# Attention and a spectral layer on four pictures: from pairs of pictures to single pictures cut in halves

## The chip, the cores and the metric

The kernel runs on one core of a Trainium2 chip. The metric is the device time of one execution in microseconds (us); of the kernel before there are three runs, with a median of 3028.91 us (3028.34 to 3029.63). The engines are PE (TensorE, matrix multiplication; PEld is its loading of weights), DVE (VectorE), ACT (ScalarE), POOL (GpSimd) and SP, which here only issues transfers.

## The reference

The input x has 4 pictures of 64 channels and 96 x 96 = 9216 pixels. All is float32. Two layers follow one another.

```python
# layer 0: x = x + scale * (attention(gn(x)) + gn(x))
q, k, v = wq x + bq, wk x + bk, wv x + bv        # 8, 8 and 64 channels
att = sigmoid(q^T k)                             # 9216 x 9216, per picture
out = v att^T + x                                # x: normalised in groups of 2 channels
scale = sigmoid(mlp(mean(out)) + mlp(max(out)))  # one number per picture and channel
# layer 1: x = x + irfft2(mix(rfft2(gn(x))))
# only 32 rows (16 lowest, 16 highest) x 16 columns of the spectrum are kept;
# each of these 512 frequencies has its own complex 64 x 64 matrix, the same for all pictures
```

The attention matrix is never stored. It has 4 x 9216 x 9216 elements, and this is nearly all of the work.

## The kernel before

**Layout.** Two pictures make a pair: 2 x 64 channels lie on the 128 partitions, and 9216 pixels along the free dimension (`xs[p]`, p = 0, 1). Queries go in blocks of 512 pixels (`NB`), 18 a pair (`NBLK`), so 36 in all. Keys go in chunks of 128 pixels, 72 a picture. A tile is 128 keys of one picture against 512 queries: 144 tiles a block (`TILES`), 5184 in all (`ALL`).

**Stream.** For each tile TensorE makes energies (`energies`, L580: 32 rows by 128 columns against 512 queries, in float32r, with key and query each split in a high and a low part), ScalarE takes the sigmoid (`sigmoids`, L601, several banks of PSUM at once), and TensorE multiplies with the values (`attend`, L618). L618 adds up a block of 64 channels per picture over 144 tiles in one bank; at the end of a block VectorE adds the result to x (L624) and takes its maximum (L626).

**The planner.** The order on the engines is written out. A loop at L805 to L877 makes bursts of up to seven tiles. In turn t the program issues the energies of burst t+1, then the values matmuls of about one burst before. Other work is hung into the turns: a step in `together` uses banks that the burst has just freed (L907, `values_of`, `keys`, `back_h`, `back_w`), a step in `alone` gets one of the two accumulating banks, and the next burst then has six tiles (L894, for `along_w`, `along_h`, `mixing`, statistics). `ends` holds what follows at the end of a turn: vector work and transfers. Where a block changes (`edges`) the burst also has six. `follow` (L718) is a queue of steps that must keep a distance of some turns.

**Keys, queries and values.** `values_of` (L489) makes, for 512 pixels of both pictures, the values and the transposed queries and keys; it has 32 matmul instructions. The parts of keys and queries are turned on VectorE (L537), sent to DRAM by SP (L541) and fetched again: queries by SP (L558), keys by POOL into `stage` (L550), from where VectorE copies them into `kT` (L552). `kT` has 18 slices of 8 tiles. The first 12 slices (`DIRECT`) of the first pair are made by TensorE itself (`keys`, L486). The second pair's values go through 9 turns with two `values_of` each, in the last block of the first pair.

**Ahead of the stream.** SP loads x in pieces of 512 KB, VectorE takes statistics of 18 blocks of the first pair (L632), normalises the first blocks (L170), and TensorE makes the first keys and queries.

**Layer 1 of the first pair** runs hidden in the stream of the second (`Hidden`, L289). In `result` the layer's input is formed in 12 strips of 8 lines; it goes to DRAM and comes back turned (`turned`). `along_w` (6 steps) is the transform along a line, `along_h` (one for each picture) along a column. `mix` (L217) multiplies each kept frequency with its matrix: pictures, real and imaginary part stand on the side that is loaded into TensorE (32 columns), and the matrices are streamed, 16 steps. `back` fetches the result in another order through DRAM, `back_h` (4 steps) and `back_w` (12 steps) are the inverse transforms.

**Layer 1 of the second pair** lies behind the stream (L928 on). From the gate on: 12 strips (L183 combine, L991 transpose, L1003 along the line, some strips added by a transfer, `ADDED`), statistics, rows in three groups (L1009, L1015), the spectrum with its scaling (L1050 to L1066), mixing of the 32 weight rows (L230; 9 come early in the stream, 6 in places free in time, 17 after the stream), `pick` (L261) which brings the last two row groups to their place by matmuls, the addition L274, the inverse along a column (L1105, L1112) and along a line (L1122), the last addition (L1130) and the output (L1131). `occupy` (L958) issues matmuls without use, so that TensorE is busy where it would wait.

Of the kernel before, what the change touches and what calls it, by code (L numbers as in the profile page):

```python
# [43 lines left out]
NPAIR = B // 2  # L44
# [5 lines left out]
NBLK = N // NB  # L50
# [7 lines left out]
ALL = NPAIR * NBLK * TILES  # L58
# [3 lines left out]
U = KH * KW * 4  # L62
UPAD = 4 * SIDE
# [3 lines left out]
NSTRIP = N // STRIP  # L67
ADDED = (4, 5, 6, 8, 10)
# [6 lines left out]
SECOND = {"w1": 2 * R, "w2": P, "ident": P, "fw": 2 * KW, "fh": 4 * KH, "gh": 2 * H, "gw": 4 * W}  # L75
# [7 lines left out]
NLATE = 3 * NSQ * P  # L83
NPICK = 2
PICK = P + 4 * (NPICK - 1)
# [3 lines left out]
def tile_kernel(ctx: ExitStack, tc: tile.TileContext, x, cst, late, spec, out):  # L89
    nc = tc.nc  # L90
    xf = x.rearrange("b c h w -> (b c) (h w)")
    outf = out.rearrange("b c h w -> (b c) (h w)")
# [8 lines left out]
    for p in range(NPAIR):  # L101
        xt = xpool.tile([P, N], F32, tag=f"x{p}", name=f"x{p}")
        for s in range(9):
            parts = 2 if p == 0 and s == 8 else 1
            for i in range(parts):
                cols = bass.ts(parts * s + i, N // 9 // parts)
                nc.sync.dma_start(xt[:, cols], xf[bass.ts(p, P), cols])
        if p == 0:
            nc.sync.dma_start(cs[:, :NFIRST], cst[:, :NFIRST])
        xs.append(xt)  # L110
    nc.sync.dma_start(cs[:, NFIRST:], cst[:, NFIRST:])

    vT = xpool.tile([P, NCH, P], F32, tag="vT", name="vT")
# [4 lines left out]
    pav, nhalf, low_sb, ident = named("pav"), named("nhalf"), named("low"), named("ident")  # L118
# [10 lines left out]
    def group_stats(stats, bank, name):  # L129
# [3 lines left out]
        mr = small.tile([P, 2], F32, tag=f"mr_{name}", name=f"mr_{name}")  # L133
        t = small.tile([P, 1], F32, tag="t", name=f"t_{name}")
        d = small.tile([P, 1], F32, tag="d", name=f"d_{name}")
# [36 lines left out]
    class Layer1:  # L172


        def __init__(self, p, gate, bank, move, queues):
            self.p, self.gate, self.bank, self.move, self.queues = p, gate, bank, move, queues
            self.vd = dram.tile([KH, 32, KW * C], F32, tag=f"vd{p}", name=f"vd_{p}")
            self.vt = None

        def combine(self, s, old):  # L180

            cols = bass.ts(s, STRIP)
            nc.vector.scalar_tensor_tensor(xs[self.p][:, cols], xs[self.p][:, cols], self.gate,  # L183
                                           old, ALU.mult, ALU.add)

        def spread(self, mr):


            p = self.p
            self.rs = small.tile([P, 3, 2], F32, tag="rs", name=f"rs_{p}")  # L190
            pr = self.bank(f"pr_{p}")
            for b in range(2):
                for part in range(2):
                    self.last = nc.tensor.matmul(pr[bass.ts(part, C), bass.ts(b, 2)],
                                                 ident[:, bass.ts(b, C)], mr,
                                                 start=True, stop=True)
            v = pr[:, :4].rearrange("q (b t) -> q t b", t=2)
            m = small.tile([P, 2], F32, tag="m", name=f"m_{p}")
            if p == 0:
                nc.vector.tensor_scalar(m, v[:, 0, :], float(-H), None, ALU.mult)  # L200
                nc.vector.tensor_copy(self.rs[:, 0, :], v[:, 1, :])
                nc.vector.tensor_scalar(self.rs[:, 1, :], v[:, 1, :], -1.0, None, ALU.mult)
# [7 lines left out]
        def constant_mode(self):  # L210

            for part in range(2):
                rows = bass.ts(part, C)
                at = self.ut[rows, 2 * part:2 * part + 2]
                nc.vector.tensor_tensor(at, at, self.rs[rows, 2, :], ALU.add)
# [1015 lines left out]
```

## Time and profile before

| what | us |
|---|---|
| median of three runs | 3028.91 |
| profiled execution, its time | 3029.19 |
| its span, first to last instruction | 3027.4 |
| first energies (L580) start | 23.4 |
| last values matmul (L618) ends | 2949.8 |
| PE busy | 3009.2 (99%) |
| ACT busy | 2416.8 (80%) |
| DVE busy | 308.1 (10%) |

The page gives busy time of each engine in 40 equal slices, the granted clock of TensorE in tenths, the load of the transfer engines, the chain of work that ended last, and groups of instructions by line. A group's row has the line, engine, operation, tiles and shapes, then the busy time, the mean of one in ns, and the idle time ahead of it with what ended it. A timeline's row has the start, the time, and the instruction with its count. [...]

### The profile page before, as it was taken

Reading aid. Unit: us, or ns where it says so; the run is one execution under the profiler, and the core shown is the slowest. Engines: PE = TensorE matmul, PEld = TensorE weight load, DVE = VectorE, ACT = ScalarE, POOL = GpSimd, SP = SyncE. Lnnn points to the kernel's source line nnn. Section 1 sums busy time; section 2 is a strip of 40 time slices with the busy share of each in tenths; the row PEclk is TensorE's granted clock in tenths of the full one; section 3 lists DMA queues with packets and bytes.
Section 4 is the critical chain, followed back from the end, with each engine's and each line's share of the span. In section 5 each row is a group of like instructions: output and inputs, shape, how many; then the busy total and the mean of one; then the engine's idle time right before and its main releaser. Section 6 shows DMA issues by size and latency. Waiting matters only on the chain.

```text
span 3027.4 us, 44108 instructions
## 1 busy us (share of the span) xinstructions
PE 3009.2 (99%) x19364; PEld 1111.5 (37%) x19364; DVE 308.1 (10%) x706; ACT 2416.8 (80%) x1555; POOL 69.8 (2%) x138
## 2 busy tenths in 40 slices
PE   9999999999999999999999999999999999999998
PEld 4333333333333333333433333333333333333336
DVE  6300000000000000002411101100000000000006
ACT  4788888888888888887788887777778888888873
POOL 0100000000000000001300000000001000000001
PEclk9999999999999999999999999999999999999999
DMA  4100000000000000001422322412113000000027
GB/s 159 32 4 4 4 4 4 4 4 4 2 4 4 4 4 4 4 4 31 99 68 64 91 79 84 135 34 46 50 47 125 4 4 4 4 4 4 1 60 252
DMA packets 114609, 117.09 MB, mean 39 GB/s; under 512 B 77488, under 2 KB 84784, under 8 KB 114320
## 3 DMA queue, kind: packets, MB, share of 16 engines
q1 hardware_dynamic: 105536, 92.82, 11.0%
q0 software_dynamic: 7472, 18.56, 2.0%
q8 instruction: 152, 2.49, 0.3%
q10 hardware_dynamic: 1408, 2.88, 0.3%
q14 instruction: 41, 0.34, 0.0%
HBM read 79.94 MB, written 32.31 MB: 37 GB/s over the span
## 4 chain that ended last, share of the span: by engine, by line
PE 98%; DVE 1%; DMA 0%; ACT 0%; issue 0%; SPq 0%; POOL 0%; DVEq 0%; ACTq 0%
PE banks L618 77%; PE banks L580 17%; PE banks L499 1%; PE banks L230 1%; PE pv L230 0%; DVE x L1130 0%; PE banks L421 0%; DMA x<-in_x_dram 0%; PE pa L1003 0%; ACT at L601 0%; PE banks L344 0%; PE pu L1015 0%; PE banks L464 0%; DVE xt L991 0%; DVE x L183 0%
## 5 line engine op out<-in xcount | busy, mean ns | idle before, releaser
L601 ACT ACTIVATE at<-banks 128x2048 f32<-128x2048 f32 (+1 forms) x1501 | 2388.3, 1642 | 533.7 <-PE banks L580 521.7
L618 PE MATMUL banks<-at,vT 128*64 128x512 f32 (+1 forms) x11824 | 2402.0, 547 | 0.0
L618 PEld LDWEIGHTS banks<-at,vT 128*64 128x64 f32 x11824 | 778.2, 136 | 1362.7 <-issue 1307.6
L580 PE MATMUL banks<-q,kT 32*128 32x512 f32 x5040 | 542.7, 452 | 0.8 <-ACT at L601 0.7
L580 PEld LDWEIGHTS banks<-q,kT 32*128 32x128 f32 x5040 | 223.7, 182 | 447.5 <-issue 333.4
L624 DVE SCALAR_TENSOR_TENSOR x<-banks,x 128x512 f32<-128x512 f32 x36 | 24.9, 691 | 2023.2 <-PE banks L618 1945.3
L550 POOL DMA_DIRECT2D stage<-qk x96 | 47.6, 503 | 932.3 <-DMA qk<-turned 929.1
L425 DVE TENSOR_TENSOR x<-banks,x 128x768 f32<-128x768 f32 x12 | 11.5, 958 | 168.5 <-PE banks L421 168.5
L499 PEld LDWEIGHTS banks<-cs,x 64*64 64x64 f32 x1152 | 21.8, 135 | 17.0 <-ACT at L601 12.8
L506 DVE TENSOR_TENSOR vT<-banks,cs 128x256 f32<-128x256 f32 x72 | 26.8, 413 | 0.0
L499 PE MATMUL banks<-cs,x 64*64 64x80 f32 (+1 forms) x1152 | 25.9, 234 | 0.0
L626 DVE TENSOR_REDUCE maxs<-x 128x1 f32<-128x512 f32 x36 | 24.7, 686 | 1.3
L632 DVE BATCH_NORM_STATS2 stats<-x 128x6 f32<-128x512 f32 x36 | 22.6, 682 | 3.7 <-DMA x<-in_x_dram 3.7
L736 DVE COPY ws<-banks 128x512 f32<-128x512 f32 x16 | 11.1, 691 | 115.3 <-PE banks L230 115.3
L163 POOL TENSOR_TENSOR mr_l<-ve_l,cs 128x1 f32<-128x1 f32 x4 | 2.2, 559 | 837.1 <-DVE ve_l L162 837.1
L736 DVE COPY ae<-banks 128x512 f32<-128x512 f32 x6 | 4.2, 692 | 157.3 <-issue 114.9
L984 POOL DMA_DIRECT2D x<-vT x5 | 4.5, 1035 | 659.5 <-ACT x L983 659.5
L580 PE MATMUL banks<-q_first,kT 32*128 32x512 f32 x144 | 17.3, 463 | 1.8 <-ACT at L601 1.1
L671 PE MATMUL banks<-x 128*128 128x256 f32 (+1 forms) x48 | 14.4, 459 | 4.7 <-DMA x<-in_x_dram 4.7
L537 DVE STREAM_TRANSPOSE turned<-t 128x384 f32<-128x384 f32 (+1 forms) x35 | 17.8, 509 | 1.2
L170 DVE TENSOR_SCALAR x<-x,mr_l 128x512 f32<-128x512 f32 x36 | 17.6, 530 | 0.7 <-POOL mr_l L163 0.7
L1003 PE MATMUL pa<-xt,lc 128*128 128x256 f32 x72 | 16.8, 385 | 0.6 <-DVE mr_l L152 0.4
(145 smaller groups left out, 425.7 us busy)
## 6 DMA issues: line engine op xcount, KB each, us to landing
ws<-in_spec_dram SPq DMA_DIRECT2D x20, 512.0 KB
q<-qk SPq DMA_DIRECT2D x280, 32.0 KB
x<-in_x_dram SPq DMA_DIRECT2D x17, 512.0 KB
out_dram<-x SPq DMA_DIRECT2D x17, 384.0 KB
room<-in_spec_dram SPq DMA_DIRECT2D x12, 512.0 KB
old<-in_x_dram SPq DMA_DIRECT2D x12, 384.0 KB
qk<-turned SPq DMA_DIRECT2D x96, 48.0 KB
x1d<-x SPq DMA_DIRECT2D x12, 384.0 KB
```

Of the source, the lines that this page charges most:

```text
L170: nc.vector.tensor_scalar(dst, src, mr[:, 0:1], mr[:, 1:2], ALU.subtract, ALU.mult)
L230: self.last = nc.tensor.matmul(pv[bass.ts(g, 32), :].rearrange("q (n k o) -> q n k o", n=SIDE, o=C)[:, :, k, :], self.ut[:, at:at + 32], s ...
L499: projected[0] = nc.tensor.matmul(pp[bass.ts(e, P // 2), b, 2 * a + h, :width], src[rows, a, h, bass.ts(e, P // 2)], named("wv")[rows, :wi ...
L506: nc.vector.tensor_tensor(vT[:, 4 * s:4 * s + 4, bass.ts(b, C)].rearrange("p (h a) m -> p a h m", h=2), pp[:, b, :, :C].rearrange("p (a h) ...
L537: nc.vector.transpose(turned[:, k:].rearrange("p k a (m h) -> p (k a) h m", h=2), t[:, k:].rearrange("p k a h m -> p (k a) h m").bitcast(F32))
L550: nc.gpsimd.dma_start(come[bass.ts(r, QK), :], split[p][s][:, r % 2, bass.ts(r // 2, NB // 2)])
L580: nc.tensor.matmul(banks[:, bank_of(i), :], kT[r:r + 32, i % TILES // 8, i // 4 % 2, :], ask[i // TILES][r:r + 32, :], start=True, stop=True)
L601: nc.scalar.activation(at[:, of:of + n, :], banks[:, bank:bank + n, :], AF.Sigmoid)
L618: attended[0] = nc.tensor.matmul(acc[half, cols], vT[:, j, half], at[:, place(2 * pair + b), cols], start=(j == 0), stop=(j == NCH - 1 and ...
L624: nc.vector.scalar_tensor_tensor(blk, acc, 1.0, blk, ALU.mult, ALU.add, accum_out=sums[p][:, m:m + 1])
L626: mark[0] = nc.vector.tensor_reduce(maxs[p][:, m:m + 1], blk, AX.X, ALU.max)
L632: each = [lambda s=s: nc.vector.bn_stats(stats[:, s, :], xs[p][:, bass.ts(s, NB)]) for s in range(NBLK)]
```

## The change

Pictures now go one by one. The upper half of a picture (48 lines) lies on partitions 0 to 63, the lower on 64 to 127, so `xs` has four tiles of 4608 columns. A block is 512 pixels of the upper half and 512 of the lower; there are 9 blocks a picture and 36 in all, each with 144 tiles of 128 keys by 512 queries as before. The key and value chunks of both halves serve both halves' queries.

Ahead of the stream only the first picture's 2.36 MB are loaded and measured, in pieces of 128 KB on SP and ACT, one for each half. Group statistics are averaged over the two halves too. `values_of` takes one block of 512 columns in both halves, that is 16 tiles' keys, and is called 9 times a picture. There are two buffers of values, so that the next picture's are written while the last is read; these calls stand one to a turn in the last block of each picture. A slice of `kT` is 256 columns in both halves, still 8 tiles; two slices come with one `values_of`, and the first 12 of the first picture are made by TensorE.

Layer 1 of pictures 0, 1 and 2 is hidden. After each of them come its gate, 6 strips, three `along_w`, statistics and one `along_h`, while the stream goes on with the next picture. The scaling needs no matmul now (`spread`). The three spectra stand side by side (`n = 3`), and one mixing of 16 steps serves all, in the stream of the last picture; 6 `back_h` and 18 `back_w` follow, three turns apart where they were four. Behind the stream is layer 1 of picture 3 alone: 6 strips, two row groups, one spectrum, a mixing of the same 32 weight rows with one picture, picks of half the width, and 6 strips of output, each written by two transfers. Of the weights 12 rows come early, 6 in places free in time, 4 into a buffer of values as the stream ends, 10 behind the strips. The matrix for the inverse comes ready from the host.

The diff is cut to its core.

```diff
-NBLK = N // NB
+NBLK = HALF // NB
+NKEY = 2 * NBLK
-ADDED = (4, 5, 6, 8, 10)
+ADDED = (4, 5)
+APART, APART_LAST = 6, 4
...
+    for p in range(B):
+        xt = xpool.tile([P, HALF], F32, tag=f"x{p}", name=f"x{p}")
+        step = NB if p == 0 else 3 * NB
+        for s in range(HALF // step):
+            cols = bass.ts(s, step)
+            read(xt[:, cols], p, cols, (nc.sync, nc.scalar if p == 0 else nc.sync))
-    vT = xpool.tile([P, NCH, P], F32, tag="vT", name="vT")
+    vTs = [xpool.tile([P, NCH, C], F32, tag=f"vT{i}", name=f"vT{i}") for i in range(2)]
...
+        def keep(self, q, queue):
+            for g in range(4):
+                queue.dma_start(self.vd[4 * q + g],
+                                self.vms[q][32 * g:32 * g + SIDE * 2 * self.n, :])
...
+        def spread(self, p, mr):
+            rs = self.rs[p] = small.tile([P, 3], F32, tag="rs", name=f"rs_{p}")
+            nc.vector.tensor_copy(rs[:, 0:1], mr[:, 1:2])
...
+        def mixing(self, q, half):
+            self.mix(q, half)
+            if half == 0:
+                return
+            self.keep(q, nc.sync)
+            if q in (5, 7):
+                first, rows = KH // 2 * (q == 7), KH // 2
+                for slot in range(2):
+                    for b in range(2):
+                        self.back(self.vt, 64 * b + 32 * slot, first, rows, b, slot, 0, SIDE, nc.sync)
+                    for n in range(2):
+                        self.back(self.vt2, 64 * n + 32 * slot, first, rows, 2, slot, 2 * n, 2, nc.sync)
...
+        NSTAGE = 8
+        stage = work.tile([P, NSTAGE, NB // 2], F32, tag="stage", name="stage")
...
             for r in range(4):
                 nc.gpsimd.dma_start(come[bass.ts(r, QK), :],
-                                    split[p][s][:, r % 2, bass.ts(r // 2, NB // 2)])
+                                    split[p][s // 2][:, r // 2, bass.ts(s % 2, NB // 2)])
...
             def means():
+                nc.vector.tensor_reduce(f[:, 1:2], maxs[p], AX.X, ALU.max)
+                nc.vector.tensor_copy(top, f[C:, 1:2])
                 nc.vector.tensor_reduce(tot, sums[p], AX.X, ALU.add)
+                nc.vector.tensor_tensor(f[:C, 1:2], f[:C, 1:2], top, ALU.max)
+                nc.vector.tensor_scalar(f[:, 0:1], tot, 1.0 / HALF, None, ALU.mult)
             def hidden():
+                nc.tensor.matmul(ph[:R, 1:2], named("w1", C), f[:C, 1:2], start=True, stop=True)
+                nc.tensor.matmul(ph[:R, 0:1], named("w1"), f[:, 0:1], start=True, stop=True)
...
+            for m in range(NSTRIP // 2):
+                follow(True, lambda m=m: l1.along_w(p, m), 1, 15 + apart * (2 * m + 1))
+            stats = l1.stats_steps(p)
+            follow(None, stats[0])
+            for step in stats[1:3]:
+                follow(True, step, 2)
+            follow(None, lambda: (stats[3](), home(p)), 2)
+            follow(True, lambda: l1.along_h(p), 2)
+            if p < HIDDEN - 1:
+                return
...
+            for i in range(6):
+                follow(2, lambda i=i: l1.back_h(i % 2, i // 2), 4 if i else 4)
+            for b in range(HIDDEN):
+                for s in range(NSTRIP):
+                    follow(2, lambda b=b, s=s: l1.back_w(b, s), 3 if b or s else 9)
...
-                if renewed < NBLK and was >= TILES * (NBLK - 1) + 8 * (renewed + 2):
-                    for s in (renewed, renewed + 1):
-                        steps.append((2, lambda s=s: values_of(1, s)))
-                        arrive(t, 1, s)
-                    renewed += 2
+                p, s = divmod(renewed, NBLK)
+                if p < B and total[t] >= TILES * (NBLK * p - 1) + 16 * (s + 1):
+                    steps.append((2, lambda p=p, s=s: values_of(p, s)))
+                    arrive(t, p, 2 * s)
+                    arrive(t, p, 2 * s + 1)
+                    renewed += 1
...
+        for i in range(4):
+            weight(next(late_rows), last_v[:, bass.ts(i, KW * C)], nc.sync)
...
             var = small.tile([P, 1], F32, tag="var", name="var")
+            rows_turned(0)
+            rows(0)
             nc.vector.tensor_reduce(var, squares, AX.X, ALU.add)
...
+        for s in range(4):
+            weight(next(late_rows), place_of(f"t{s}", f"w_t{s}"), nc.sync)
+        for i in range(4):
+            weight(next(late_rows), again[:, bass.ts(i, KW * C)], nc.sync)
+        for n in range(NGROUP):
+            weight(next(late_rows), place_of(f"a{n}", f"w_a{n}"), nc.sync)
...
+        nc.vector.tensor_tensor(vt, picked, vt, ALU.add)
+        occupy(1, l1.last, mix_bank.tile([P, NB], F32, tag="v", name="idle_v", bufs=6), NB // 2)
...
+                write(p, cols, x1[:, cols], (nc.sync, nc.scalar))
```

## The prediction

> **What bounds the kernel now.** I read the page's busy slices and its chain first, then the timeline of one engine to get the price of a turn, then a table of stages for the end.
>
> ```profile
> PE   9999999999999999999999999999999999999998
> PE 98%; DVE 1%; DMA 0%; ACT 0%; issue 0%; SPq 0%; POOL 0%; DVEq 0%; ACTq 0%
> L618 PE MATMUL banks<-at,vT 128*64 128x512 f32 (+1 forms) x11824 | 2402.0, 547 | 0.0
> ```
>
> TensorE is never free and 98% of the chain is its own. So in the stream nothing is hidden: a step that puts work on TensorE costs its time, and one that only adds DMA, VectorE (10% busy) or GpSimd work costs nothing unless TensorE waits for it. Only ahead of the stream (to 23.4 us) and behind it (from 2949.8 us) do other engines set the pace. The timeline gives the price of a turn (energies of one burst, then the values matmuls of the one before) as the distance between the starts of two bursts:
>
> ```profile
> 2937.22 0.73 PE L580 MATMUL banks<-q,kT 32*128 32x512 f32 x7
> 2941.05 0.73 PE L580 MATMUL banks<-q,kT 32*128 32x512 f32 x7
> ...
> 94.23 0.74 PE L580 MATMUL banks<-q_first,kT 32*128 32x512 f32 x7
> 96.77 0.79 PE L499 MATMUL banks<-cs,x 64*64 64x80 f32 x32
> 98.92 0.73 PE L580 MATMUL banks<-q_first,kT 32*128 32x512 f32 x7
> ...
> 1402.07 0.74 PE L580 MATMUL banks<-q,kT 32*128 32x512 f32 x7
> 1404.61 1.34 PE L499 MATMUL banks<-cs,x 64*64 64x80 f32 x64
> 1407.32 0.73 PE L580 MATMUL banks<-q,kT 32*128 32x512 f32 x7
> ...
> 1564.07 0.73 PE L580 MATMUL banks<-q,kT 32*128 32x512 f32 x6
> 1564.74 1.06 PE L344 MATMUL banks<-xT,cs 96*32 96x512 f32 x8
> 1568.46 0.74 PE L580 MATMUL banks<-q,kT 32*128 32x512 f32 x7
> ```
>
> A plain turn of seven tiles takes 3.82 us. One of six at an edge takes 3.39, so a tile is 0.43 and the fixed part of a turn 0.81. Every step has a price above that: one `values_of` beside the burst 0.87 (98.92 - 94.23 - 3.82), two in one turn 1.44, an `along_w` alone 1.00 (4.39 - 3.39). Read the same way at every turn: `mixing` 1.00, `along_h` 1.85, `back_h` 1.21, `back_w` 0.98, `hidden` and `gates` 0.40 and 0.11, the two statistics steps of layer 0 0.31 each, of layer 1 0.67 and 0.93, `spread` 0.23, keys with values 1.45. Turns with no step at all hold 6.2 us of small stalls together. With these prices the 751 turns add up to the stream.
>
> **The change, part by part.** Work is counted by walking the planner's loop, in the old and the new form.
>
> *Tiles and turns.* 36 query blocks of 144 tiles both times, so the 5184 x 0.43 us stay. 46 steps now take a burst of six for themselves instead of 31, edges stay 35: 753 turns for 751, **+1.6** (2 x 0.81).
>
> *Values and keys of the first image.* The first pair had 18 `values_of` in its first 15 turns, at 21.7 us above plain turns. The first image has 9 (one ahead, eight here). Turns: first two as before (2.8 and 2.3, they wait for ScalarE), four with keys and values (4 x 1.45), four with keys alone (1.45 - 0.87, with the burst's split 0.65 each), two with values alone (0.87): 15.2. **-6.5.**
>
> *Values of the later images.* Before, 18 in nine turns of two: 13.0. After, 27 singles in 27 turns. A single has 0.79 us of matmul, but costs 0.87. 27 x 0.87 = 23.6: **+10.6.** If a single cost only half a pair (0.72) it would be +6.5; I take the measured single.
>
> *Hidden spectral layer.* Three images for two. `along_w` 9 for 6 (+3.0), `along_h` 3 for 2 (+1.9), `back_h` 6 for 4 (+2.4), `back_w` 18 for 12 (+5.9), layer-0 statistics 3 x 2 steps for 2 (+1.2), gates three times with one more tiny matmul (0.15) each (+1.5). Layer-1 statistics run three times, `spread` leaves TensorE. Their one execution came to 1.6 us, but one step waited for a bank at an edge; between 0.31 and 0.93 a step I take 0.5: 3.0 against 1.8, +1.2. `mixing` stays at 16 turns: three images widen the stationary side, not what streams. Together **+17.1** (15 to 20). DMAs: `keep` still issues four per row group, `back` eight for four, each write two for one, all on SP, whose issues take 0.3 to 0.5 us; in the same stage it waits 14 us at a time for weights and no burst suffers.
>
> *Small stalls.* About 0.1 an edge, as now; those behind the one change of pair (turns 366 to 397, 1.8 us) may come three times: **+2.8** (0 to 6).
>
> *Ahead of the stream.*
>
> ```profile
> 4.54 11.46 DVE L632 BATCH_NORM_STATS2 stats<-x 128x6 f32<-128x512 f32 x18 [3.67 <-DMA x<-in_x_dram]
> ...
> 26.00:27.00 1.00, 1.00 (x7) 0.49 (x7) 0.93 (x5) 0.89 (x2) 0.00 (x0) 0.84 1.05 411
> 27.00:28.00 1.00, 1.00 (x4) 0.30 (x4) 0.22 (x1) 1.00 (x2) 0.00 (x0) 0.50 0.56 216
> ```
>
> VectorE works without a gap from 4.54, 0.64 us a block, so 18 blocks end at 16.0. Nine take 5.7. The first piece is a quarter as large (about 0.6 us earlier); loads at the 405 GB/s seen now need 5.8 us for 2.36 MB, and the constants 0.8 more, which arrive together with the last sums, at about 9.8. The chain from there to the first energies (16.0 to 23.4) stays, with 0.2 less in the aggregate. **-6.4** (-5.5 to -7).
> [...] No row here has pieces that small in such numbers, but in the window 3.5 to 20 us pieces of 256 and 512 KB kept 401 to 425 GB/s with many in flight.
>
> *Behind the stream.*
>
> ```profile
> 2949.80:2953.00 3.20, 2.26 (x11) 1.20 (x10) 1.96 (x8) 0.20 (x1) 0.00 (x0) 1.00 0.47 123
> 2953.00:2963.10 10.10, 9.71 (x37) 6.69 (x37) 9.86 (x15) 9.96 (x18) 6.23 (x9) 1.00 0.78 139
> 2963.10:2974.10 11.00, 10.81 (x49) 7.92 (x47) 10.60 (x11) 5.65 (x12) 2.69 (x5) 1.00 1.03 318
> 2974.10:2982.70 8.60, 8.43 (x40) 4.31 (x41) 4.89 (x13) 2.74 (x8) 1.29 (x3) 1.00 1.03 410
> 2982.70:2996.70 14.00, 14.00 (x257) 9.97 (x257) 7.68 (x14) 5.79 (x10) 0.95 (x1) 1.00 0.98 376
> 2996.70:3002.90 6.20, 4.56 (x21) 3.35 (x19) 1.42 (x4) 0.58 (x1) 0.00 (x0) 1.00 0.23 64
> 3002.90:3009.50 6.60, 6.60 (x40) 4.36 (x40) 4.90 (x8) 0.00 (x0) 0.00 (x0) 1.00 0.00 0
> 3009.50:3021.40 11.90, 10.85 (x97) 10.61 (x96) 10.63 (x13) 0.00 (x0) 0.00 (x0) 1.00 0.77 294
> ```
>
> Columns: stage and length, busy time of PE, PEld, DVE, ACT, POOL, clock, DMA share, GB/s.
> Gate: two more VectorE steps of 0.2 and a second small matmul and its step, 3.2 becomes 3.9 (+0.7). Strips 0 to 5 are the second row and stay (10.1). The third row, strips 6 to 11, goes (-11.0). Spectrum (8.6): the first group's transpose (1.2) now lies behind the last strip, two row matmuls of 1.75 us follow each group, one transpose and smaller scalings replace two of each: 8.8 (+0.2). Mixing streams the same weights: 14.0. Fourteen weight rows load behind the stream for seventeen, 7.3 MB, 18 us at 410 GB/s; the last are wanted 37 us in. Picking (6.2): one addition of 0.69 for four (1.42), and half the matmuls: 5.2. Back along h (6.6): half the matmuls and four transposes of 0.62: 4.3. Strips (11.9, 0.82 to 0.95 each): 6.2. The writes run at 394 GB/s and end 6.0 us behind the last addition, where they are backed up; 2.36 MB need 6.0 us from the first and the same 2.9 of finishing, so 5.2. Sum of the last four: 30.7 becomes 20.9, -9.8. Together **-19.9** (-17 to -22).
>
> **Sum:** +1.6 - 6.5 + 10.6 + 17.1 + 2.8 - 6.4 - 19.9 = -0.7 us on the profiled execution's 3029.19 (span 3027.4 and 1.8 around it): 3028.5. The median of the runs shown is 0.3 below that execution, so I forecast a median of **3028.2**. The bounds of the terms, not all at one end, make it 3022.5 to 3034. What is taken off both ends is paid back in the stream, because the third hidden image and the single `values_of` lie on the engine that is full.
>
> **Where a clock rule bears.** The two rows at 26 and 27 us show the granted clock at 0.50 for one stretch of 3.4 us after TensorE had been busy 0.63, 0.85 and 0.09 of three seconds; eight values matmuls took 3.36 us for 1.94. The shorter tail has fewer matmuls to keep it busy, above all the 2.8 us between the picks and the vt addition. One such stretch there costs at most 1.7 us.
> [...]
>
> **Rivals.**
> *Faster:* the cheap ends of the terms. Singles at 0.72 (-4.1), layer-1 statistics at 0.31 (-1.1), no stalls more than now (-2.8): -8.0, so 3020. For it: these are pure matmul times. Against: four singles at 0.87 in the trace, none lower, and small stalls at every kind of edge.
> *Slower, the round trip of the first image's last keys:* slices 12 to 17 go through DRAM, now two to each `values_of` and the second 2 us later (four GpSimd issues, 2.0 to 2.2 us). From the start of turn 9 to VectorE's copy the trace shows 16.2 us (74.4 to 90.6). Turns get shorter, so the slice is wanted after 18.3, 17.0 and 16.2 us (before 19.8, 18.8, 17.0). If the trip takes more than about 17 us, each microsecond delays TensorE, up to three times; at 20 us 1.7 + 3.0 + 3.8 = 8.5: 3037.
> *It does not shorten the tail as meant:* the late weights or the one accumulated strip arrive late, since 2.1 MB start loading just as the stream ends. DMA was 0.98 to 1.03 busy from 2963 to 2997. Half of the eleven microseconds of the third row lost: 3034.
>
> **Chances.** Forecast 0.55, faster 0.15, key trip 0.17, late weights 0.13. A measurement of this kernel can tell about 0.2% (6 us: 3022.9 and 3035.0) from no change. Faster by more: 0.13 of the second case and 0.03 of the first. Slower by more: 0.16 of the key trip, 0.04 of the late weights, 0.02 of the first. Same: 0.62. Range 3021 to 3037: it takes in the forecast's bounds and most of every rival.
>
> **What would show it.** First energies near 17 us, the last values matmul near 2969 (2949.8 - 6.4 + 25.6, the stream's terms), and a tail of 58 us for 77.6. A single `values_of` turn at 4.69. Energies waiting for kT in turns 13 to 18 would show the key trip; a gap inside the mixing, the late weights; a clock below 0.9 in the last 60 us, the throttle. The forecast is wrong if a turn without a step is often longer than 3.83, or if `back_w` every third turn, for every fourth, waits for its load.

## The result, and the profile after

The changed kernel takes 3045.78 us (median; 3044.78 to 3047.77), the kernel before 3028.62 in the same comparison: 1.0057 times as long, 95% interval 1.004 to 1.0074. That is 17 us slower and outside the range. The profiled execution took 3046.73 us with a span of 3044.6. The page's line of busy slices and its chain:

```profile
PE   7999999999999999999999999999999999999997
PE 97%; DMA 1%; issue 0%; DVE 0%; ACT 0%; SPq 0%; ACTq 0%; POOL 0%; DVEq 0%
```

The two ends show it: the first slice fell from 9 to 7, the last from 8 to 7, and the chain of what ended last now holds 1% of DMA, which is the loads of x. The middle is as full as before. So what PE waits for lies in the first 76 us and the last 76 us, where other engines set the pace; how long the middle is, such shares do not tell.

Read turn by turn, against the prediction's terms (spans; a minus is sooner than before):

| | predicted | measured |
|---|---|---|
| first energies | 17.0 (-6.4) | 21.25 (-2.15) |
| turn 3, a turn without a step | 3.82 | 15.51 (+11.7) |
| rest of the stream, first energies to last values matmul | +25.6 | +20.8 |
| last values matmul to the end | 57.7 (-19.9) | 64.4 (-13.2) |

(The stream took 2926.4 before and 2958.9 after, 32.5 more, of which 11.7 is turn 3.) The four measured sum to the 17.2 us by which the span grew.

**Turn 3.** The timeline of three engines (start, length, engine, line, tiles, count; in brackets how long the engine had stood idle and what released it):

```profile
9.70 23.51 SPq L99 DMA_DIRECT2D x<-in_x_dram  x18
36.16 10.30 SPq L517 DMA_DIRECT2D qk<-turned  x8
40.52 0.50 PE L556 MATMUL banks<-q_first,kT 32*128 32x512 f32 x4
47.04 0.48 DVE L452 TENSOR_SCALAR full_k<-banks,cs 128x256 f32<-128x256 f32 x1 [10.57 <-DMA qk<-turned]
47.58 0.79 PE L556 MATMUL banks<-q_first,kT 32*128 32x512 f32 x1 [6.56 <-DVE full_k L452]
56.02 0.73 PE L556 MATMUL banks<-q_first,kT 32*128 32x512 f32 x7
```

Read it backwards. The burst that starts at 40.52 stops after four matmuls and waits 6.56 us for the next keys. Those come from VectorE, whose `full_k` had itself waited 10.57 us, not for data but for its buffer: `key_splits` takes its tile from the tag `turned`, two buffers that it shares with `values_of`, and the write `qk<-turned` that still reads one of them had not landed. The block's four writes were issued on SP between 36.16 and 41.13, and the last landed at 46.86, because ahead of them on SP stood 18 loads of the second to the fourth image. What SP waited for says why they took so long (us in total, times, longest):

```profile
SPq L99 <- DMA x<-in_x_dram: 15.9, 14, 2.6
SPq L517 <- DMA x<-in_x_dram: 7.9, 7, 1.4
```

Loads wait for earlier loads to land, and seven of the writes of keys do too. The records of the trace show which. Each transfer names a semaphore that its landing raises; in this trace all 871 transfers of SP and ACT share eight of them (numbers 99 and 101 to 107), strictly in turn up to 3014 us, and in the head each is issued only when the transfer that last had its semaphore has landed. The load issued at 21.35 waits for the load of 11.49, which lands at 21.33, and the first write, at 36.16, for the load of 21.35, which lands at 36.08. So no more than eight transfers of these two queues are under way at once here, and a write of 16 KB waits for a load of 384 KB eight places ahead. The idle PE then costs once more: the granted clock is 0.50 from 45.56 to 55.80, where two kernels without the stall (one transfer, loads put off, both below) have 1.00 from 42 to 56 us.

**The loads.** The same columns as in the tables of stages ahead: start and end, length, busy PE, PEld, DVE, ACT, POOL, clock, DMA share, GB/s. First the kernel before, then after:

```profile
12.00:16.00 4.00, 3.84 (x18) 2.83 (x17) 4.00 (x7) 0.00 (x0) 0.00 (x0) 1.00 1.05 401
```
```profile
13.00:17.00 4.00, 3.44 (x15) 2.09 (x14) 1.14 (x6) 0.00 (x0) 0.52 (x1) 1.00 1.05 246
30.00:35.00 5.00, 5.00 (x53) 2.08 (x52) 3.38 (x12) 2.81 (x2) 0.00 (x0) 1.00 1.02 234
```

The DMA engines are full in all three rows (share 1.0), but move 234 to 246 GB/s instead of 401. A full engine that moves little over half as much is not short of work; each packet takes it longer (6 KB in 428 ns, median of 15 to 33 us, for 236 in the kernel with one transfer below).

**Behind the stream,** by the stages of the prediction (gate; strips and spectrum in two rows; mixing; picks; back along h; strips; end):

```profile
2980.10:2983.90 3.80, 2.44 (x13) 1.34 (x12) 2.31 (x11) 0.20 (x1) 0.00 (x0) 1.00 0.64 230
2983.90:2994.10 10.20, 10.20 (x35) 7.00 (x35) 9.97 (x15) 7.72 (x14) 1.92 (x3) 0.83 1.06 299
2994.10:3004.40 10.30, 8.53 (x28) 4.87 (x27) 4.78 (x13) 1.24 (x2) 0.56 (x1) 1.00 0.97 372
3004.40:3018.50 14.10, 14.07 (x258) 10.03 (x260) 6.50 (x10) 4.11 (x8) 0.53 (x1) 1.00 0.41 86
3018.50:3025.50 7.00, 2.71 (x19) 1.20 (x19) 0.69 (x1) 0.59 (x1) 0.00 (x0) 0.99 0.12 30
3025.50:3031.70 6.20, 5.56 (x20) 3.81 (x20) 2.51 (x4) 0.00 (x0) 0.00 (x0) 0.73 0.00 0
3031.70:3039.10 7.40, 5.25 (x96) 3.85 (x96) 5.62 (x7) 0.00 (x0) 0.00 (x0) 1.00 0.58 168
3039.10:3044.60 5.50, 0.00 (x0) 0.00 (x0) 0.00 (x0) 0.00 (x0) 0.00 (x0) 0.81 0.61 207
```

The third row of strips did go. But the picks took 7.0 us for 5.2, with PE busy in 2.71 of them, and back along h 6.2 for 4.3, at a mean clock of 0.73. The addition to `vt` waits for its reads from DRAM, and SP's reads wait for ACT's (the waits of SP in that stage):

```profile
3024.69 0.69 DVE L1104 TENSOR_TENSOR vt<-picked,vt 128x512 f32<-128x512 f32 x1 [6.32 <-DMA vt<-vd]
...
3025.48 3.67 PE L1114 MATMUL pz_last<-vt,lc 64*128 64x256 f32 x16 [4.18 <-DVE vt L1104]
```
```profile
SPq L242 <- DMA vt<-vd: 4.1, 2, 3.9
```

ACT issues its four reads of `vt` from 3019.24 on, SP its four only from 3021.19 on. SP's first two carry the same semaphores as ACT's first two and go out when these have landed (3021.00 and 3021.74).

### The profile page after: what moved, and what is told of

Read it like the earlier page. It is cut to its first block, busy times and chain, and to the rows that moved or that the text cites. A ratio compares the mean times of both kernels' runs of the same rounds, so it can differ in the third digit from the quotient of the medians.

```text
span 3044.6 us, 44711 instructions
## 1 busy us (share of the span) xinstructions
PE 3012.3 (99%) x19368; PEld 1097.0 (36%) x19368; DVE 338.1 (11%) x818; ACT 2406.3 (79%) x1539; POOL 135.2 (4%) x275
## 4 chain that ended last, share of the span: by engine, by line
PE 97%; DMA 1%; issue 0%; DVE 0%; ACT 0%; SPq 0%; ACTq 0%; POOL 0%; DVEq 0%
PE banks L594 77%; PE banks L556 16%; DMA x<-in_x_dram 1%; PE banks L475 1%; PE banks L220 1%; PE banks L399 0%; PE pv L220 0%; PE banks L305 0%; ACT at L577 0%; PE pa L1011 0%; PE banks L371 0%; DMA qk<-turned 0%; PE banks L333 0%; PE idle L970 0%; PE banks L441 0%
## 5 line engine op out<-in xcount | busy, mean ns | idle before, releaser
L526 POOL DMA_DIRECT2D stage<-qk x240 | 117.9, 499 | 959.1 <-DMA qk<-turned 951.4
L403 DVE TENSOR_TENSOR x<-banks,x 128x768 f32<-128x768 f32 x18 | 17.2, 958 | 212.5 <-PE banks L399 201.4
L475 PEld LDWEIGHTS banks<-cs,x 64*64 64x64 f32 x1152 | 22.8, 136 | 27.3 <-ACT at L577 25.3
L492 DVE TENSOR_TENSOR u<-banks,cs 128x128 f32<-128x128 f32 x35 | 10.2, 290 | 189.8 <-PE banks L475 189.8
L744 POOL DMA_DIRECT2D w_early<-in_spec_dram x12 | 6.4, 543 | 521.7 <-PE banks L399 357.5
L608 DVE BATCH_NORM_STATS2 stats<-x 128x6 f32<-128x512 f32 x36 | 23.4, 680 | 6.1 <-DMA x<-in_x_dram 6.0
L185 DVE SCALAR_TENSOR_TENSOR x<-x,gate,old 128x768 f32<-128x768 f32 x18 | 18.2, 1009 | 17.7 <-DMA old<-in_x_dram 17.7
L273 DVE STREAM_TRANSPOSE old<-x 128x768 f32<-128x768 f32 x18 | 17.6, 978 | 0.6
```

Of the source, the lines that this page charges most:

```text
L185: nc.vector.scalar_tensor_tensor(xs[p][:, cols], xs[p][:, cols], gate, old, ALU.mult, ALU.add)
L475: projected[0] = nc.tensor.matmul(pp[bass.ts(e, P // 2), b, 2 * a + h, :width], src[rows, a, h, bass.ts(e, P // 2)], named("wv")[rows, :wi ...
L526: nc.gpsimd.dma_start(come[bass.ts(r, QK), :], split[p][s // 2][:, r // 2, bass.ts(s % 2, NB // 2)])
L608: each = [lambda s=s: nc.vector.bn_stats(stats[:, s, :], xs[p][:, bass.ts(s, NB)]) for s in range(NBLK)]
```

## Experiments

**The theory.** Transfers that write 64 partitions move a little over half of what those to 128 move (234 to 246 GB/s above, for 401). By that the head is longer than forecast, the loads of x1 to x3 hold SP's queue until 36 us, the writes of keys behind them are late, and the shared buffer carries this to VectorE and TensorE. **Rivals:** the pieces are too small (128 and 384 KB for 512); the queue or the buffer alone would do it at any rate; in the tail, the number of DMA issues or the clock rather than the order of the reads.

### Halves in the kernel before

```
-                nc.sync.dma_start(xt[:, cols], xf[bass.ts(p, P), cols])
+                for e in range(2):
+                    nc.sync.dma_start(xt[bass.ts(e, C), cols], xf[bass.ts(2 * p + e, C), cols])
```

> The kernel before with every load of x split into two transfers of 64 partitions, both on SP; nothing else changes. Theory (a transfer to 64 partitions runs at a little over half the rate: 235 GB/s in the profile of after against 405 in that of before): the first pair's 4.7 MB take some 20 us instead of 11.7, so the first energies come some 8 us later (23.4 to about 31.5), the second pair's loads end near 47 us, and the key writes behind them on SP come late too, which may add up to another 10: 3037 to 3049 us. Rival (the smaller pieces or the dearer issue, not the halves): pieces of 256 KB are no smaller than the last two of before, which ran at the full rate, so the rate stays near 400 and the time within 2 us of 3029.

Measured: 3043.5 us, 1.0052 times the kernel before (1.0037 to 1.0067), so +15.4 from this edit alone. That it is close to the whole loss of the change is chance: the parts differ. First energies come at 31.32 us (23.40 before), 7.9 later, where the change loses 2.95 to the halves. The table of stages of this kernel, while the first image pair loads:

```profile
7.00:10.00 3.00, 2.52 (x6) 1.18 (x4) 1.29 (x2) 0.00 (x0) 0.00 (x0) 1.00 1.05 240
```

240 GB/s for 401, the engines as full as before, with pieces of 256 KB. In the trace's packet records a packet of 4 KB takes 287 ns (median, 12 to 16 us) where the kernel before has 165. The second part of the loss is the stall again:

```profile
44.98 0.51 PE L581 MATMUL banks<-q_first,kT 32*128 32x512 f32 x4
55.97 0.74 PE L581 MATMUL banks<-q_first,kT 32*128 32x512 f32 x7
```

This turn takes 10.99 us, for 5.28 in the kernel before. In it VectorE waits 4.2 us for a write of keys to land, and the granted clock is at 0.50 for 6.83 us.

### One transfer for both halves in the kernel after

The input is sent in another order of memory, so that image, half and channel give 128 rows at an even distance.

```
-        for e in range(2):
-            queues[e].dma_start(to[bass.ts(e, C)], xf[p][e, :, cols])
+        queues[0].dma_start(to, xf[p][:, cols])
...
-        "x": given["x"],
+        "x": given["x"].reshape(B, C, 2, H // 2, W).transpose(0, 2, 1, 3, 4),
```

> After, with x sent from the host in the order image, half, channel, row, so that each piece of a picture is one transfer of 128 partitions in place of two of 64 (the first image's pieces alternate between SP and ACT; the computation is the same, only the order of the input in memory differs, and no work on the device replaces it). Theory: the loads run near 405 GB/s, x1 to x3 (7.1 MB) are in before 32 us instead of 41, the key writes land in time, the stall of 11.7 us in turn 3 is gone, and the first energies come at 17 to 18.5 instead of 21.2: 3029.5 to 3033 us. Rival (the load's rate has nothing to do with the stall, or the head is bound by work on DVE): either stays, 3041 to 3046.

Measured: 3029.89 us (1.0006 of before, 0.9996 to 1.0015), 15.9 below after. First energies 18.30. From its table and its timeline:

```profile
7.00:10.00 3.00, 3.00 (x12) 2.47 (x11) 2.84 (x6) 0.00 (x0) 0.00 (x0) 1.00 1.07 400
12.00:16.00 4.00, 3.77 (x15) 2.08 (x14) 1.74 (x7) 0.47 (x1) 0.55 (x1) 1.00 1.02 421
```
```profile
37.58 0.74 PE L555 MATMUL banks<-q_first,kT 32*128 32x512 f32 x7
41.40 0.73 PE L555 MATMUL banks<-q_first,kT 32*128 32x512 f32 x7
```

In the first row the pieces have 256 KB, the size that ran at 240 GB/s in halves, and move at 400; in the second they have 768 KB. The size is not the cause. Nor is it the length of a row: a packet of 6 KB takes 236 ns here and 428 in after (medians, 10 to 24 and 15 to 33 us). Nor is it the order of the input in memory, which this edit changes too: in the kernel before that order was left alone, and halving by itself brought the rate down. Turn 3 (37.58 to 41.40) takes 3.82 us. The loads alone carry 2.95 us of the head and all 11.7 of the stall.

### Which link carries the stall: queue, other queue, buffer

Three edits of after, each at the halved rate. The first takes the loads of x1 to x3 out of the head:

```
-            read(xt[:, cols], p, cols, (nc.sync, nc.scalar if p == 0 else nc.sync))
+            if p == 0:
+                read(xt[:, cols], p, cols, (nc.sync, nc.scalar))
...
+            if 17 <= t < 26:
+                p, cols = 1 + (t - 17) // 3, bass.ts((t - 17) % 3, 3 * NB)
+                end(t, lambda p=p, cols=cols: read(xs[p][:, cols], p, cols, (nc.sync, nc.sync)))
```

> After, with the loads of the second to the fourth image taken out of the head and issued on SP in turns 17 to 25 of the stream, so that the first writes of the split keys find SP's queue empty. Theory (the stall of 11.7 us in turn 3 is DVE's, whose key tile shares a buffer with tiles that those writes still read): the turn is 3.8 us again, 3032 to 3036 us, the first energies at 20 to 21.2. Rival (the stall is one of work or of buffers by themselves): 3044 to 3047.

Measured: 3034.89 us, 10.9 below after.

```profile
41.30 0.74 PE L557 MATMUL banks<-q_first,kT 32*128 32x512 f32 x7
45.12 0.73 PE L557 MATMUL banks<-q_first,kT 32*128 32x512 f32 x7
```

Turn 3 takes 3.82 us; first energies 22.32, a microsecond later than in after and outside what I had expected.

The second leaves the loads and moves the writes:

```
-                    nc.sync.dma_start(
+                    (nc.gpsimd if p == 0 and s < 4 else nc.sync).dma_start(
                         split[p][s][:, k:].rearrange("r k (a g m) -> g r (k a) m", a=2, g=4)[g],
```

> After, with the writes of the split keys of the first image's first four blocks on POOL's queue instead of SP's, so that they don't wait behind the 18 loads there but still share the DMA engines with them. Theory A (the order within SP's queue is what delays them): the stall of turn 3 shrinks from 11.7 to 0 to 3 us, 3034 to 3038. Theory B (the engines are full until 41 us, whichever queue the write is on): it stays above 8 us, 3042 to 3047.

Measured: 3038.33 us, 7.5 below after.

```profile
41.80 0.50 PE L556 MATMUL banks<-q_first,kT 32*128 32x512 f32 x4
48.24 0.73 PE L556 MATMUL banks<-q_first,kT 32*128 32x512 f32 x7
```

Turn 3 is 6.44 us long, a stall of 2.6 for 11.7. So most of it is the place behind the loads, and a quarter is left when the same transfers only share full engines. In the trace of after POOL's transfers have eight semaphores of their own (111 to 118), so on that queue these writes wait for no load; on ACT's queue, which shares SP's eight, they might have. That was not tried.

The third leaves loads and queues and gives the tiles room:

```
-                turned = qp.tile([P, 3, 2, NB // 8], F32, tag="turned", name=f"turned_{p}_{s}")
+                if p == 0:
+                    turned = vTs[1].rearrange("p n c -> p (n c)")[:, bass.ts(s, 6 * NB // 8)] \
+                        .rearrange("p (k a m) -> p k a m", k=3, a=2)
+                else:
+                    turned = qp.tile([P, 3, 2, NB // 8], F32, tag="turned", name=f"turned_{p}_{s}")
```

> After, with the turned tiles of the first image's nine blocks each in a place of its own (in the second image's values tile, which is empty then), so that the full keys share no buffer with them; loads and queues as in after. Theory (DVE's key tile waits only because its buffer is still read by writes that stand behind the loads on SP): the stall of 11.7 us in turn 3 is gone although the writes land as late as before, 3033 to 3036 us. Rival (something else needs those writes by turn 3, or the loads slow the keys by themselves): 3040 to 3047.

Measured: 3034.13 us, 11.7 below after. Its timeline:

```profile
35.71 17.22 SPq L521 DMA_DIRECT2D qk<-vT  x16
41.60 0.74 PE L560 MATMUL banks<-q_first,kT 32*128 32x512 f32 x7
45.43 0.73 PE L560 MATMUL banks<-q_first,kT 32*128 32x512 f32 x7
```

The writes are as late as in after (35.71) and take until 53 us, and turn 3 is 3.83 us all the same: nobody needs what they carry yet. The stall needs all three links, the slow loads, the place behind them and the shared buffer, and cutting any one ends it or most of it.

### Both halves at once

```
-            read(xt[:, cols], p, cols, (nc.sync, nc.scalar if p == 0 else nc.sync))
+            read(xt[:, cols], p, cols, (nc.sync, nc.scalar if p == 0 else nc.gpsimd))
```

> After, with the upper halves of the second to the fourth image loaded from POOL's queue and the lower ones from SP's, so that both halves of the partitions are written at the same time. [...] Theory B (transfers to 64 partitions stay slow side by side as well; the first image's halves, on SP and ACT, ran at 230 to 281 GB/s): 235 to 280 GB/s, loads in at 37 to 41 us, the stall 6 us or more, 3039 to 3046.

(In the code it is the lower halves, on partitions 64 to 127, that go to POOL.)

Measured: 3050.73 us, slower than after by 5. While both halves are written the rate, 239 to 268 GB/s, is about what Theory B expected; the time lies over its 3046, and the stall it expected is gone. From its table:

```profile
10.00:14.00 4.00, 1.22 (x2) 0.50 (x2) 0.69 (x1) 0.00 (x0) 0.00 (x0) 1.00 1.06 268
30.00:36.00 6.00, 5.92 (x29) 3.61 (x30) 2.69 (x9) 1.23 (x3) 0.56 (x1) 1.00 1.02 206
```

The two rows are of different things. Between 10 and 26 us the packets are of all three queues, POOL's for one half and SP's and ACT's for both, and the rows read 239 to 268 GB/s: queues for both halves at once do not add up to the 400 of one transfer to both. POOL's end by 26 us. From 27 to 43 us every packet of the loads is of SP's queue, which now loads one half only, and the rate is 206: that is one half alone, with 482 ns for a packet of 6 KB. In after, where SP's loads go to the two halves in turn, it is 234 to 246. I had overlooked that POOL has nothing else to do at the start. It issued its nine loads by 8.4 us, they shared the engines with the first image, and the first energies came at 37.06. Turn 3 takes 3.82 us: the price was paid ahead of the stream.

### The tail

Four edits on top of the kernel with one transfer, whose head is clean. `vt` in the table is the start of its addition after the first matmul of the last mixing.

The reads of `vt`, first four on POOL as soon as their blocks are kept, last four on SP:

```
-            for first, rows_of, behind in ((0, 16, last - 1), (16, 16 - 4 * NPICK, last)):
+            for first, rows_of, behind, queue in ((0, 16, 4, nc.gpsimd),
+                                                  (16, 16 - 4 * NPICK, last, nc.sync)):
...
-                                        2 * half, 2, (nc.scalar, nc.sync)[slot])
+                                        2 * half, 2, queue)
```

> The kernel of e2_one_transfer with the eight reads of vt at the end of the last mixing put on other queues: the first four (rows 0 to 15) on POOL as soon as their blocks are kept, the last four all on SP, none on ACT. Theory (in after, SP's four wait 3.5 us for ACT's four to land, since they write the same tile from another queue): vt's addition comes 1.5 to 3.5 us sooner after the last matmul on the values than in e2_one_transfer, and with the shorter pause the clock may hold through pz, another 1.5: a tail of 57.5 to 61 us against 62.5, 3025 to 3029 us. Rival (the landing of the last kept block sets it, not the order of the reads): within 0.5 us of 62.5.

One transfer for each q in `keep`:

```
-            for g in range(4):
-                queue.dma_start(self.vd[4 * q + g],
-                                self.vms[q][32 * g:32 * g + SIDE * 2 * self.n, :])
+            queue.dma_start(self.vd[4 * q:4 * q + 4].rearrange("h s m -> (h s) m"), self.vms[q])
```

> The kernel of e2_one_transfer with the last image's mixed blocks kept by one transfer of 128 partitions for each q (32 rows for each line of the spectrum, of which 8 are used, four times the bytes) in place of four of 8 partitions: 6 issues on SP for 24. Theory (the number of issues delays the last keep, and with it the reads of vt): vt's addition 0.5 to 1.5 us sooner, tail 60.5 to 62 us against 62.5. Rival (the wait between the reads' two queues is all of it, or the four times larger transfer takes the gain back): 62 to 63.5.

More idle matmuls ahead of `pz`:

```
-        occupy(1, l1.last, mix_bank.tile([P, NB], F32, tag="v", name="idle_v", bufs=6), NB // 2)
+        occupy(4, l1.last, mix_bank.tile([P, NB], F32, tag="v", name="idle_v", bufs=6))
```

> The kernel of e2_one_transfer with four idle matmuls of 512 columns behind the picks in place of one of 256, so that PE's pause before pz is 1.4 us instead of 3.4 (vt is added at the same time). Theory (pz runs at half clock only because PE paused): its 16 matmuls take 1.7 to 1.9 us instead of 3.3, tail 60.5 to 61.3 us against 62.5. Rival (the clock falls anyway, for want of load over the whole stage): tail 62.3 to 62.7.

The first two together, with a fuller gate (`for n in (NB, NB)` at line 922), and the first one with the fuller gate alone:

> The kernel of e2_one_transfer with the edits of e5_back_queues and e6_keep_one together, and a fill of two matmuls of 512 columns in place of one of 512 and one of 256 behind the last matmul on the values. Theory (with the reads of vt on two queues that don't wait for each other, what is left is the landing of the last kept block, which one transfer brings sooner): vt's addition 0.3 to 0.8 us sooner than in e5_back_queues, tail 58.7 to 59.5 us against 59.6, 3025 to 3027 us and under the kernel before by 0.05 to 0.15%. Rival (the larger transfers take it back): 59.6 to 60.5, 3026.5 to 3028.

> The kernel of e5_back_queues with a fill of two matmuls of 512 columns in place of one of 512 and one of 256 behind the last matmul on the values; blocks kept by four small transfers for each q as in after. Theory (in e9_tail_all the four times larger last block, landing late under POOL's reads, took back more than the fewer issues saved, while the reads' order by itself is worth 3 us): vt's addition 17 to 18 us after the first matmul of the last mixing, as in e5_back_queues (17.5), a tail of 59 to 60 us, 3025.5 to 3027.5 us and 0.03 to 0.12% under the kernel before. Rival (e5_back_queues had its clock by luck, and the order is worth less): a tail over 61 us, 3028 to 3030, no faster than before.

| kernel | us (median) | last values to mixing | `vt` | tail |
|---|---|---|---|---|
| after | 3045.78 | 24.3 | 20.25 | 64.4 |
| one transfer | 3029.89 | 23.4 | 19.43 | 62.5 |
| and reads of `vt` moved | 3026.46 | 23.4 | 17.52 | 59.6 |
| and `keep` as one transfer | 3028.18 | 23.4 | 18.35 | 62.1 |
| and more idle matmuls | 3028.04 | 24.3 | 19.41 | 61.9 |
| and reads, `keep` and gate | 3029.47 | 23.4 | 18.98 | 62.3 |
| and reads and gate | 3026.24 | 23.4 | 17.56 | 59.5 |

With the reads moved `vt` comes 1.9 us sooner, and tail and time lie where the theory put them. Where SP waits now, and `vt` and `pz` in that kernel:

```profile
SPq L241 <- DMA vd<-w_early: 1.7, 4, 0.7
```
```profile
3005.71 0.69 DVE L1104 TENSOR_TENSOR vt<-picked,vt 128x512 f32<-128x512 f32 x1 [3.58 <-DMA vt<-vd]
```
```profile
3006.51 2.19 PE L1114 MATMUL pz_last<-vt,lc 64*128 64x256 f32 x16 [1.45 <-DVE vt L1104]
```

SP waits for the last kept block only. The theory's reason, that the reads write the same tile from two queues, does not hold: POOL's and SP's do so too, and SP's first goes out at 3002.89, while POOL's last lands at 3003.34. With reads and gate it goes out at 3001.99, before any of POOL's has landed (3002.22). What differs is the semaphores: POOL has its own, ACT and SP share theirs. That this alone is the cause was not tested.

The shorter pause (1.45 us) also keeps the clock: `pz` takes 2.19 us, for 3.81 behind a pause of 3.36 in the kernel with one transfer. The idle matmuls give the same without touching the reads:

```profile
3008.66 2.09 PE L1113 MATMUL pz_last<-vt,lc 64*128 64x256 f32 x16 [0.34 <-PE idle_v L969]
```

So the clock in `pz` hangs on PE's pause, and is worth 1.7 us in that step. The other profiles agree: behind pauses of 2.28 to 4.45 us the clock fell in all nine, behind 0.34 to 1.50 in none of three. The median fell by 1.9. In the profiled execution the tail is only 0.6 shorter, because it fell to half clock at the gate as well (24.3 for 23.4 in the table).

`keep` as one transfer brought `vt` 1.1 us sooner, as its theory expected, but the tail is 62.1, as its rival did: `pz` is at half clock still (3.80 us), and 0.7 is lost behind it for a reason that was not looked for.

The combination failed. It went the way of its rival, but further: a tail of 62.3 us and a time of 3029.47 lie outside both. With `keep` as one transfer the last block is four times as large and lands beside POOL's reads (the waits of SP):

```profile
SPq L246 <- DMA vd<-w_early: 4.1, 2, 3.4
```

From the first issue of the last block to SP's next read it is 4.7 us here, 3.9 with the large block and no reads by POOL, and 3.5 with small blocks and POOL's reads. The large block is the slower one, and most so beside POOL's reads.

Dropping that edit gives 3026.24 us, 0.9991 of before with an interval of 0.9982 to 1.0. It is the best of these kernels, but what is left of the gain cannot be told from none with certainty, and it needs the input in another order. That the fuller gate does anything is not shown by the times: 23.4 with and without it.

Without the new order of the input, the kernel with the loads put off and all three edits of the tail:

> The kernel of e3_loads_later (half transfers, but off the head's queue) with the same three edits of the tail as e9_tail_all. If the tail's gain is independent of the head, 3034.9 less 3 to 5 us: 3030 to 3032; what is left above e9_tail_all is then the head with its half transfers, 4 us.

Measured: 3033.42 us, 1.0013 of before (1.0004 to 1.0022), 1.5 below the same without the edits of the tail, less than expected. It holds the larger `keep`, which took back the gain in the combination above; without it this kernel was not run.

## Why the prediction was wrong

The step that failed is the price of a load, which also put the wait on loads in the stream at nothing. It stood in two places.

*Ahead of the stream:* "loads at the 405 GB/s seen now need 5.8 us". That row was of transfers to 128 partitions, and the change writes 64 at a time. The first image's last sum is taken at 13.05 us in after, at 10.40 with one transfer, 9.8 forecast; first energies 21.25, 18.30, 17.0. Of the miss of 4.25 us, 2.95 are the halves; the remaining 1.3 are the sums 0.6 later and the chain behind them 0.7 longer than I put it.

In the runs one half alone moved 206 GB/s and transfers to 128 partitions 400 to 421; the 234 to 246 of after are with loads to both halves under way on one queue. I had weighed the size of the pieces and not the half that they write; the runs show that at 256 KB the size was not what counted (240 GB/s in halves, 400 in one transfer). Nor do two queues for the two halves make up for it: both together moved 239 to 268 GB/s, more than the 206 of one, but far from 400. What holds a half back no run shows.

*In the stream:* "one that only adds DMA … costs nothing unless TensorE waits for it". True, and I did not follow who might wait. I counted the loads of the first image and left out that the next three stand on the same queue ahead of the writes of keys, and that these hold buffers of VectorE. The rival I named for the keys (turns 13 to 18, the round trip through DRAM) did not happen; those turns are 3.82 us long or have the price of their step. The stall came ten turns earlier, from the same writes, through the buffer instead of the data. The prediction's own sign, a turn without a step longer than 3.83, is what showed it.

*The rest of the stream* was right in its mechanism. Single `values_of` 0.878 each (0.87 forecast), 23.7 together. (Such a call issues 16 matmul instructions, not 32; the trace has 32 records of them, two for each.) `along_w`, `along_h`, `mixing`, `back_h`, `back_w` at 0.99, 1.85, 1.00, 1.18 and 0.98 us as priced. Layer-1 statistics 0.31 a step, not 0.5, and gates and `hidden` a little cheaper; the first turns a little dearer (0.785 for keys alone, 0.65 forecast). Small stalls 5.5 to 7 us, by the turn to which an edge is counted, for 9.0. Together 4.8 below the sum.

*Behind the stream:* 64.4 for 57.7. From the last values matmul to the mixing 24.3 for 22.8: 0.9 of it is a half-clock stretch at the gate: kernels that did not fall there have 23.4; the other 0.6 was not taken apart. Picks +1.8: SP's reads of `vt` wait for ACT's, and moving them won back 1.9. Back along h +1.9, of which the clock is 1.5 to 1.6, as the prediction's weighing of the clock had allowed (up to 1.7) but not counted. Strips and end +1.5 together. No late weights: the mixing took 14.05.

*The clock.* What the prediction read from its row (a fall after a stretch with PE partly busy; its 0.63, 0.85 and 0.09 are of three microseconds) held: in the 3.41 us ahead of the fall at 2984.44 PE was busy 2.06. The same stage fell in the profiles of after and of three of the other kernels with it, and not in those of eight (three of these with the fuller gate). The stretches between two changes of the clock are whole multiples of 3.413 us in these traces. Counted back in steps of 3.413 us from a later change of the clock, the window that holds the gate's pauses had PE busy 2.06 to 2.08 us in the four that fell and 2.17 or more in the eight others. In one of these, the kernel with reads and gate, it lies as in the four, and the fuller gate makes it 2.48; there the fill may have kept the clock. A threshold does not follow: ahead of `pz`, windows with 1.92 and 1.97 did not fall.

What stays open: strips and end of the tail, 1.5 us, were not tried apart, and the semaphores were read from the trace, not varied. Nor was another order of the partitions, by which a picture of the unchanged input could be read in one transfer.

## What to carry to other kernels

A layout that splits a tile over the halves of the partitions is not free because the bytes stay the same (here 206 to 246 GB/s for 400): read the GB/s beside the DMA share, and take the price of a load from a row with the same partitions. For every transfer that gets slower, list what is issued behind it, also on another queue that shares its semaphores (SP's first read of `vt` was held 3.9 us by ACT's), and for each of those which buffer it holds and who wants that buffer next; the stall here was one of room, while the data was not needed until later.

## What the runs showed that I had not expected

- DMA engines at a share of 1.0 move 206 GB/s in transfers to one half of the partitions, 234 to 246 in transfers to the two halves in turn on one queue, and 400 to 421 in transfers to 128; at 256 KB a piece it is 240 and 400.
- Queues that write the two halves at the same time reach 239 to 268 GB/s, little more than one queue that writes them in turn.
- SP and ACT share eight semaphores for their landings in these traces (99 and 101 to 107 in after), and a transfer waited until the one that last had its semaphore had landed: SP's first read of `vt` was held 3.9 us by ACT's, and writes of 16 KB by loads eight places ahead.
- Every stretch between two changes of the clock in these traces is a multiple of 3.413 us long (at 0.50 they have 3.41, 6.83 and 10.24). At the gate, whose pauses hardly differ, the clock fell in four profiles of twelve and cost 0.9 us each time.
